# A graph network on one core: the preparation in another order, thresholds inside the norm's steps, and one visit instead of two for a gathered block's rows

## The chip, the cores and the metric

The kernel runs on one core of a Trainium2 chip. The metric is the device time of one execution in microseconds (us). TensorE is called PE (its weight loads PEld), VectorE DVE, ScalarE ACT, GpSimd POOL, SyncE SP.

## The reference

A layer norm without gain and bias, a ReLU, four rounds of "add the neighbours, then a small network", and the input added back. There are N = 6250 nodes with C = 256 channels and E = 100000 edges, sorted by their target `dst`.

```python
def agg(h):
    return jax.ops.segment_sum(h[src], dst, num_segments=N)
for l in range(NL - 1):                      # NL = 4
    h = x + agg(x)
    h = relu(h @ W1s[l] + b1s[l])
    h = relu(h @ W2s[l] + b2s[l])
    x = h @ W3s[l] + b3s[l]
h = x + agg(x)
h = relu(h @ cW1 + cb1)                      # 256 to 256
h = relu(h @ cW2 + cb2)                      # 256 to 64
return h @ cW3 + cb3                         # 64 to 256

# around it
h = relu(layernorm(x))
return x + gnn(h, ...)
```

## The kernel before

All is float32 in and out. The 6250 nodes are 49 blocks of 128 (`NT`). Since no nonlinearity stands between one layer's third product and the next layer's first, these two weights are multiplied ahead (`fused`, W3 times W1), and what a layer stores to its `table` in DRAM is already multiplied for the next aggregation. The work with sorted edges is in `sorted_edges`; a second way, for unsorted edges, is behind a condition and isn't run.

An aggregation is done in two ways. For most blocks a matrix of edge counts (source by target, uint8) is multiplied with the node table that stands in SBUF. For the blocks in `gone` the table's rows are gathered by GpSimd with an indirect DMA (L1382, one DMA for 128 rows, 17 of them a block, `T = 17`), and PE sums them with one-hot matrices `hot` (L1402) in narrow products of 32 targets (L1419). There are 82 such sums over the four layers (23, 20, 20, 19), with 391, 340, 340 and 323 gathers.

*Preparation* (0 to 126 us). Three generators are stepped by hand, so that the order of their `next` calls is the order of the instructions on each engine's queue:

- `look` works out where edges start. It loads every 128th target (L620, cast at L644), counts how many lie below each of 98 half blocks (L652 to L661), gathers for each half block the near edges (L663, 1408 of them, `NEAR`), and counts those below 17 thresholds 4 nodes apart: 11 on DVE (L695) and 6 on ACT by a sign with a sum (L698, `Sign`), ahead of the norm. From the counts it works out `first` and `starts` (L704 and on) and queues 32 gathers (`asks`), which `ask(n)` issues. Later stages build `idx` (the sources to gather) and `rel` (targets relative to the block).
- `normed` is the layer norm over 25 pairs of blocks in 30 steps: x loads in groups of 6 blocks, `moments` (L879), square roots for 6 blocks at a time (L885), `scale` (L899), transposes (L908), the product with the first weights (L920), and the table's parts `XY` (L936, L940).
- `fused` makes the products of weights, with a copy of a bias on POOL (L579).

`load_biases` issues bias loads on ACT's queue (L538, L541), and `load_w` the weights (L527). `wrong` is a small tile in which flags of unsorted edges are collected; it is cleared on DVE (L640).

*Layer 0* (from 126 us). `build` makes the count matrices: per step two one-hots, `lo` and `hi` (L1035, DVE), two products (L1076), and a cast of the counts to uint8, in turn on ACT (L1084) and DVE (L1086). The first `PRE` = 12 ticks of two steps run before the first product of the layer (to 142.7 us). Layer 0 then multiplies node block by node block (L1588), and stores the matrices, which layers 1 to 3 load again panel by panel (L1665).

*Gathered blocks* (class `Gathered`). A planner counts the time of the work issued on PE in a clock of its own (`clock`). A layer's gathers are issued evenly over it (`flow`, `send`), starting `LEAD` = 21 ahead of the first visit, into 24 buffers in layer 0 and 25 after it. A "visit" is a group of the L1419 products between two stretches of other products. `ROUNDS` gives two visits to a block: rows `c + 4 m` with c in (3, 1, -1), then with c in (0, 4, 2). `hot` has two buffers; that of the next visit is made right behind a visit. After a block's second visit, `finish` adds the sums to the block (L1448) and goes on with its small network.

The planner's price of a visit is `VISIT` = 1.7.

Of the kernel before, what the change touches and what calls it, by code (L numbers as in the profile page):

```python
# [8 lines left out]
F32 = mybir.dt.float32  # L9
# [387 lines left out]
def sorted_edges(  # L397
# [59 lines left out]
    ROUNDS = ((3, 1, -1), (0, 4, 2))  # L457
# [3 lines left out]
    NEAR = 11 * P  # L461
# [36 lines left out]
    rel = const.tile([P, left[NQ] // T, len(ROUNDS), 3, P // Q], BF16, name="rel")  # L498
# [58 lines left out]
    def fused(pool, w3_aps, w1_aps):  # L557
# [11 lines left out]
        for l in range(NLAYER):  # L569
# [8 lines left out]
            b3b = pool.tile([P, KC, P], F32, name="b3b", bufs=1)  # L578
            nc.gpsimd.tensor_copy(b3b, b3[l][:, :, None].to_broadcast([P, KC, P]))  # L579
            yield  # L580
            w = pool.tile([P, KC + 1, C], F32, name="w31", bufs=1)
            for i in range(KC + 1):
                ps = ps_m.tile([P, W], F32, name="ps")
                for k in range(KC):
                    left = w3t[:, k, i * P:(i + 1) * P] if i < KC else b3b[:, k, :]
                    nc.tensor.matmul(ps[:, :C], left, w1[:, k, :], start=(k == 0),
                                     stop=(k == KC - 1))
                nc.scalar.copy(w[:, i, :], ps[:, :C])
# [28 lines left out]
    def look(pool):  # L617
        firsts_i = pool.tile([1, EB], I32, name="near_i", bufs=1)
        with nc.allow_non_contiguous_dma(reason="each tile's first destination"):
# [6 lines left out]
        nc.sync.dma_start(out=run[:FULL, :], in_=bass.AP(tensor=dst.tensor, offset=dst.offset,  # L626
                                                         ap=[[EC, FULL], [1, EC + 1]]))
        nc.sync.dma_start(out=run[FULL:FULL + 1, :E - FULL * EC],
                          in_=dst[FULL * EC:E].rearrange("(o e) -> o e", o=1))
# [15 lines left out]


        half = pool.tile([P, 2], F32, name="half", bufs=1)
        junk = pool.tile([P, NEAR], BF16, name="junk", bufs=1)
        for h in range(2):
# [3 lines left out]
                             start=True, stop=True)  # L653
            nc.vector.tensor_scalar(junk[:NSUB, e0:e1], ps[:NSUB, :e1 - e0], low[:NSUB, 0:1], None,
# [11 lines left out]
        )  # L666
        yield
# [24 lines left out]
        DV = 11  # L692
        for q in range(GSUB + 1):
            if q < DV:
                nc.vector.tensor_scalar(junk[:NSUB], near[:NSUB], float(GD * q), None,  # L695
                                        op0=OP.is_lt, op1=OP.add, accum_out=less[:NSUB, q:q + 1])
            else:
                nc.scalar.activation(junk2[:NSUB], near[:NSUB], AF.Sign, bias=edge[:NSUB, q:q + 1],  # L698
                                     accum_out=less[:NSUB, q:q + 1])
                yield  # L700
        nc.vector.tensor_scalar(less[:NSUB, DV:], less[:NSUB, DV:], -0.5, float(NEAR // 2),
                                op0=OP.mult, op1=OP.add)
        first = pool.tile([P, GSUB + 1], F32, name="first", bufs=1)
        nc.vector.tensor_scalar(first[:NSUB], less[:NSUB], at[:NSUB, 0:1], None, op0=OP.add)  # L704
        starts = pool.tile([NSUB, GSUB], I32, name="starts", bufs=1)
        nc.vector.tensor_scalar(starts, first[:NSUB, :GSUB], float(E - P), None, op0=OP.min)
        wd = pool.tile([P, GSUB, P], I32, name="wd", bufs=1)
        ws = pool.tile([P, GSUB, P], I32, name="ws", bufs=1)
        for q in range(GSUB):
            for w, e in ((wd, dst), (ws, src)):  # L710
                asks.append((w[:NSUB, q, :], e, starts[:, q:q + 1]))
        ask(4)
# [4 lines left out]
        sel = pool.tile([P, NQ, PW], F32, name="near_i", bufs=1)  # L717
# [100 lines left out]
        for w, (q0, q1) in ((3, (0, NQ - 1)), (4, (NQ - 1, NQ))):  # L818
            rows = gone[q0][1] * T
            nc.vector.tensor_reduce(wrong[:rows, w:w + 1], off[:rows, q0:q1, :],  # L820
                                    axis=mybir.AxisListType.XY, op=OP.max)
        ask(len(asks))
# [8 lines left out]
        yield  # L831
        for t, o in ((fd, rel), (fs, idx)):
# [4 lines left out]
            if o is rel:  # L837
                v = ps[:, :left[NQ]].rearrange("p (b k) -> p b k", k=T)
                for i, rounds in enumerate(ROUNDS):
                    for c in rounds:  # L840
                        g = 1 if c < 0 else 0
                        nc.vector.tensor_scalar(o[:, :, i, (c - min(rounds)) // 2, g:],
# [16 lines left out]
    def normed(pool, ps_t, ps_z):  # L859
        G = 6  # L860
# [91 lines left out]
        settle(G)  # L952
        yield
        for s in range(len(pairs) + 5):
            if s % (G // 2) == 0 and s and s * 2 + 3 * G < NT:
                load(s * 2 + 3 * G)
            for lag, f in ((3, out), (4, high), (0, scale), (1, turn), (2, times), (-G, moments),
                           (4, low), (5, keep)):
                if 0 <= s - lag < len(pairs) and (f is not moments or s - lag >= G):
                    f(s - lag)  # L960
            settle(s + G - 1)
            yield

    with tc.manual_schedule():
        with tc.tile_pool(name="prep", bufs=2) as prep, tc.tile_pool(
# [5 lines left out]
            next(rows)  # L971
            make_identity(nc, ident)
            nc.vector.memset(eps, EPS)
            turn_biases, (b1, b2, b3) = load_biases(prep)
            ahead_w = fused(prep, [W3s[l] for l in range(NLAYER)],
                            [W1s[l + 1] for l in range(NLAYER - 1)] + [cW1])
            next(ahead_w)
            next(looked)
            for t, pattern in ((cols, [[1, NT], [STEP, GD]]), (lanes, [[1, P]]), (colf, [[1, P]])):
                nc.gpsimd.iota(t, pattern=pattern, base=0, channel_multiplier=0,  # L980
                               allow_small_or_imprecise_dtypes=True)
            next(looked)
            next(rows)
# [70 lines left out]
        def build(hots, ats, ps_b):  # L1054
# [7 lines left out]
            for k, (s, q0) in enumerate(batches):  # L1062
# [6 lines left out]
                for q in range(0, BATCH, 2):  # L1069
# [13 lines left out]
                    if step % 2:  # L1083
# [251 lines left out]
        class Gathered:  # L1335
            def __init__(self, l):
# [11 lines left out]
                self.rows, self.us = {}, []  # L1348
# [49 lines left out]
            def one_hots(self, v):  # L1398
                g, rounds = self.visits[v]
                shape = [P, len(rounds), P // Q, Q]  # L1400
                self.hot = work.tile(shape, F32, name="hot", bufs=2)
# [6 lines left out]
            def add(self):  # L1408
# [4 lines left out]
                if v == 0:  # L1413
                    self.one_hots(0)
                end = rounds == ROUNDS[-1]
                for c in rounds:
                    for m in range(P // Q):
                        if c + 4 * m >= 0:
                            nc.tensor.matmul(  # L1419
                                self.sums[m * Q:(m + 1) * Q, :C],  # L1420
                                self.hot[:, (c - min(rounds)) // 2, m, :], self.rows[g, c + 4 * m],
# [367 lines left out]
```

## Time and profile before

| | us |
|---|---|
| median of 3 runs | 2130.42 |
| lowest and highest | 2127.44, 2132.5 |
| the profiled execution | 2135.8 |
| its span in the trace | 2134.0 |
| its granted clock of TensorE, mean | 0.988 of full |

The profile is of one execution. A line of a group reads: source line, engine, operation, output and inputs with shapes, count, then busy time in us, mean ns of one, and the engine's idle time just before, with what ended it. A line of the timeline reads: start and length in us, engine, line, operation, count, and in brackets the idle time before it and what it waited for. Windows give each engine's busy time and instruction count, the granted clock, the share of time that the DMA engines were busy, and GB/s.

### The profile page before, as it was taken

To read this page: it belongs to the slowest core of one execution; us is meant where nothing else is said; L and a number is where in the kernel's file an instruction comes from. 1 tells how busy PE (TensorE), PEld (TensorE's weight loads), DVE (VectorE), ACT (ScalarE), POOL (GpSimd) and SP (SyncE) were. 2 spreads that over 40 slices of the span, in tenths; PEclk is the share of its full clock that TensorE was granted. 3 is DMA by queue.
4 is the path that set the end of the run, shared out by engine and by line. 5 is a ranking of instruction groups with operands and counts; after the bars stand their busy time and mean duration, and the time that the engine had idled before them with its cause. 6 is when DMAs were issued, how large, how long until landed. Compare 5 with 4: busy or idle time off the path is not lost.

```text
span 2134.0 us, 33393 instructions
## 1 busy us (share of the span) xinstructions
PE 2057.4 (96%) x12076; PEld 1487.8 (70%) x12076; DVE 937.7 (44%) x2192; ACT 864.3 (41%) x1775; POOL 1445.4 (68%) x1470
## 2 busy tenths in 40 slices
PE   4979999999999999999999999999999999999997
PEld 3756766667667777777776777777776777777675
DVE  7877867667673422222233322222233433333332
ACT  4856655556556522323232433222333432223231
POOL 2727777777774477777776377777776277777773
PEclk9979999999999999999999999999999999999999
DMA  5524545545455655455455554555456555556553
GB/s 157 176 98 139 162 142 153 158 140 164 150 158 152 213 163 155 153 181 164 142 186 167 173 160 148 173 165 169 146 168 195 170 172 181 184 180 194 183 160 119
DMA packets 184901, 347.61 MB, mean 163 GB/s; under 512 B 32446, under 2 KB 118496, under 8 KB 184726
## 3 DMA queue, kind: packets, MB, share of 16 engines
q0 software_dynamic: 68960, 185.41, 29.7%
q1 hardware_dynamic: 113838, 158.12, 22.3%
q8 instruction: 97, 1.59, 0.3%
q10 hardware_dynamic: 1928, 1.85, 0.3%
q14 instruction: 78, 0.64, 0.1%
HBM read 287.98 MB, written 57.26 MB: 162 GB/s over the span
## 4 chain that ended last, share of the span: by engine, by line
PE 88%; DVE 5%; DMA 4%; issue 1%; ACT 1%; POOL 1%; SPq 0%; DVEq 0%; POOLq 0%; ACTq 0%
PE agg L1665 43%; PE agg L1588 16%; PE sums L1419 11%; PE ps L1233 6%; PE ps L1290 6%; PE bp L1076 4%; DMA rows<-table,idx 3%; PE ps L1479 1%; POOL rows L1382 1%; DVE junk L695 1%; PE bp L920 1%; DVE hi L1035 1%; DVE at L1086 1%; PE ps L1245 0%; DMA table<-zs 0%
## 5 line engine op out<-in xcount | busy, mean ns | idle before, releaser
L1382 POOL DMA_INDIRECT rows<-table,idx x1394 | 1387.7, 995 | 611.4 <-issue 220.6
L1665 PE MATMUL agg<-a,XY 128*128 128x512 f32 x4116 | 982.8, 395 | 1.9 <-DVE clT L1600 1.9
L1665 PEld LDWEIGHTS agg<-a,XY 128*128 128x128 f32 x4116 | 764.6, 188 | 209.5 <-issue 45.8
L1565 ACT CAST a<-at 128x512 fp32r<-128x512 uint8 (+1 forms) x542 | 326.9, 616 | 576.9 <-PE agg L1665 543.9
L1565 DVE CAST a<-at 128x512 fp32r<-128x512 uint8 x543 | 242.7, 448 | 552.8 <-PE agg L1665 469.3
L1588 PE MATMUL agg<-XY,a 128*128 128x512 f32 x1470 | 404.9, 409 | 1.3 <-DVE un L1600 0.7
L1588 PEld LDWEIGHTS agg<-XY,a 128*128 128x128 f32 x1470 | 258.9, 189 | 53.7 <-issue 8.7
L1419 PE MATMUL sums<-rows,hot 128*32 128x256 f32 x3772 | 256.0, 385 | 16.2 <-DMA rows<-table,idx 15.0
L1419 PEld LDWEIGHTS sums<-rows,hot 128*32 128x32 f32 x3772 | 112.6, 109 | 142.6 <-issue 53.6
L1549 ACT CAST a<-at 128x512 fp32r<-128x512 uint8 (+2 forms) x362 | 196.7, 574 | 6.5 <-PE agg L1588 6.5
L1084 ACT CAST at<-bp 128x392 uint8<-128x392 f32 x240 | 116.6, 487 | 203.7 <-PE bp L1076 191.0
L1086 DVE CAST at<-bp 128x392 uint8<-128x392 f32 x240 | 135.1, 563 | 138.2 <-PE bp L1076 138.2
L1448 DVE TENSOR_TENSOR u<-u,sums 128x256 f32<-128x256 f32 x82 | 34.3, 419 | 241.8 <-PE agg L1665 226.9
L1076 PE MATMUL bp<-hi,lo 128*128 128x196 bf16 x960 | 127.5, 255 | 11.0 <-DVE hi L1035 10.7
L1290 PE MATMUL ps<-w,h 128*128 128x256 f32 x588 | 133.9, 379 | 1.4 <-ACT h L1236 0.9
L1233 PE MATMUL ps<-h,w 128*128 128x512 f32 (+3 forms) x332 | 133.9, 545 | 0.6 <-DVE zz L1298 0.6
L1035 DVE TENSOR_TENSOR hi<-cols,pairs 128x784 bf16<-128x784 bf16 x240 | 134.3, 560 | 0.0
L1076 PEld LDWEIGHTS <-lo 128*128 128x128 bf16 x960 | 70.6, 99 | 81.9 <-DVE hi L1035 27.8
L1290 PEld LDWEIGHTS ps<-w,h 128*128 128x128 f32 x588 | 111.1, 190 | 18.7 <-ACT h L1236 1.8
L1483 ACT ACTIVATE h<-ps,bias 128x256 f32<-128x256 f32 (+1 forms) x116 | 47.2, 464 | 154.9 <-PE ps L1479 154.9
L1298 DVE TENSOR_TENSOR zz<-ps,w 128x512 f32<-128x512 f32 (+1 forms) x75 | 50.1, 678 | 117.0 <-PE ps L1290 117.0
L1035 DVE TENSOR_TENSOR lo<-lanes,pairs 128x512 bf16<-128x512 bf16 x240 | 100.3, 418 | 1.3 <-ACT pairs L1030 1.3
(171 smaller groups left out, 989.7 us busy)
## 6 DMA issues: line engine op xcount, KB each, us to landing
at<-mat SPq DMA_DIRECT2D x151, 448.0 KB
mat<-at SPq DMA_DIRECT2D x30, 784.0 KB
rows<-table,idx POOLq DMA_INDIRECT x1394
table<-zz SPq DMA_DIRECT2D x72, 256.0 KB
back<-table SPq DMA_DIRECT2D x99, 128.0 KB
xs<-in_x_dram SPq DMA_DIRECT2D x8, 768.0 KB
table<-zs SPq DMA_DIRECT2D x24, 256.0 KB
out_dram<-zz SPq DMA_DIRECT2D x24, 256.0 KB
```

The costliest lines, as they stand in the source:

```text
L1035: nc.vector.tensor_tensor(o.rearrange("p q (n t) -> p q n t", t=2), values.rearrange("p (n t) -> p n t", t=2)[:, None, :, :].to_broadcast( ...
L1076: mm = nc.tensor.matmul(bp[:, m * HW:(m + 1) * HW], lo[:, q + m, :], hi[:, q + m, :], start=True, stop=True)
L1084: nc.scalar.copy(o, v)
L1086: nc.vector.tensor_copy(o, v)
L1233: mm = nc.tensor.matmul(ps[:mp, :w], weights[l][0][:, c, i * P:i * P + mp], h1[:, c, :w], start=(c == 0), stop=(c == KC - 1))
L1290: mm = nc.tensor.matmul(o, h2[0][:, c, nodes], w3[:, c, :], start=(c == 0), stop=(c == KC - 1))
L1382: got = nc.gpsimd.indirect_dma_start(out=t, out_offset=None, in_=tables[self.l][:, :], in_offset=bass.IndirectOffsetOnAxis(ap=idx[:, o:o + ...
L1419: nc.tensor.matmul(self.sums[m * Q:(m + 1) * Q, :C], self.hot[:, (c - min(rounds)) // 2, m, :], self.rows[g, c + 4 * m], start=(c == ROUND ...
L1549: nc.scalar.copy(a[:, i * m * P:(i + 1) * m * P].rearrange("p (j d) -> p j d", j=m), counts[b][:, j:j + m, :])
L1565: cast(o, at[:, :, d:d + m * P])
L1588: mm = nc.tensor.matmul(agg, a[:, d:d + P], XY[:, j, :], start=(j == 0), stop=(j == NT - 1))
L1665: mm = nc.tensor.matmul(agg[c][:, :w], XY[:, j, o:o + P], a[:, :w], start=(j == 0 and half == 0), stop=(j == NT - 1 and half == 1))
```

## The change

- `ROUNDS` has one round of all six values of c: a gathered block is summed in one visit with 46 passes. `hot` has 6 x 4 x 32 columns and one buffer, and is made four pieces of work behind the visit (`later(4, ...)`). The planner's constants are LEAD 32 and VISIT 3.0, and a layer's first `send` is of 8 tiles.
- The near edges are 1280 for each half block. 8 thresholds are counted on DVE and 9 on ACT, one pair in each of the first steps of the norm; behind every four, `settled` works out their starts and queues their gathers.
- x is loaded for two groups first, and for two more after the first moments; moments run 4 pairs ahead, not 6. The loads of the edges `run` stand behind the gather of the near edges.
- The weights' loads stand ahead of the biases' on ACT's queue. A square root into `wrong`, ahead of its clearing on DVE, loads the ACT function table early.
- The bias copies on POOL are gone (the product reads the bias by broadcast). The products of weights are spread over the first norm steps, as are the steps of `look` (`STAGES`).
- In `build`, all casts of the first 24 steps are on ACT.

```diff
-    ROUNDS = ((3, 1, -1), (0, 4, 2))
+    ROUNDS = ((3, 1, -1, 0, 4, 2),)
-    NEAR = 11 * P
+    NEAR = 10 * P
...
-            b3b = pool.tile([P, KC, P], F32, name="b3b", bufs=1)
-            nc.gpsimd.tensor_copy(b3b, b3[l][:, :, None].to_broadcast([P, KC, P]))
...
-        DV = 11
-        for q in range(GSUB + 1):
-            if q < DV:
-                nc.vector.tensor_scalar(junk[:NSUB], near[:NSUB], float(GD * q), None,
-                                        op0=OP.is_lt, op1=OP.add, accum_out=less[:NSUB, q:q + 1])
-            else:
-                nc.scalar.activation(junk2[:NSUB], near[:NSUB], AF.Sign, bias=edge[:NSUB, q:q + 1],
-                                     accum_out=less[:NSUB, q:q + 1])
-                yield
...
-        ask(4)
+        def settled(q0, q1):
+            odd = slice(q0 + 1 - q0 % 2, q1, 2) if q1 <= GSUB else slice(q0, q1)
+            nc.vector.tensor_scalar(less[:NSUB, odd], less[:NSUB, odd], -0.5, float(NEAR // 2),
+                                    op0=OP.mult, op1=OP.add)
+            nc.vector.tensor_scalar(first[:NSUB, q0:q1], less[:NSUB, q0:q1], at[:NSUB, 0:1], None,
+                                    op0=OP.add)
+            if q1 > GSUB:
+                return
+            nc.vector.tensor_scalar(starts[:, q0:q1], first[:NSUB, q0:q1], float(E - P), None,
+                                    op0=OP.min)
+            for q in range(q0, q1):
+                for w, e in ((wd, dst), (ws, src)):
+                    asks.append((w[:NSUB, q, :], e, starts[:, q:q + 1]))
+
+        for q in range(0, GSUB, 2):
+            nc.vector.tensor_scalar(junk[:NSUB], near[:NSUB], float(GD * q), None,
+                                    op0=OP.is_lt, op1=OP.add, accum_out=less[:NSUB, q:q + 1])
+            for k in (q + 1,) if q + 2 < GSUB else (q + 1, q + 2):
+                nc.scalar.activation(junk2[:NSUB], near[:NSUB], AF.Sign, bias=edge[:NSUB, k:k + 1],
+                                     accum_out=less[:NSUB, k:k + 1])
+            if q % 4 == 2:
+                settled(q - 2, q + 2)
+            if q + 2 < GSUB:
+                yield
...
     def normed(pool, ps_t, ps_z):
-        G = 6
+        G, LEAD = 6, 4
...
-        for t0 in range(0, 4 * G, G):
+        for t0 in (0, G):
             load(t0)
         yield
-        for s in range(G):
+        moments(0)
+        yield
+        for t0 in (2 * G, 3 * G):
+            load(t0)
+        for s in range(1, LEAD):
             moments(s)
...
             next(rows)
+            ahead_w = fused(prep, [W3s[l] for l in range(NLAYER)],
+                            [W1s[l + 1] for l in range(NLAYER - 1)] + [cW1])
+            next(ahead_w)
             make_identity(nc, ident)
             nc.vector.memset(eps, EPS)
             turn_biases, (b1, b2, b3) = load_biases(prep)
-            ahead_w = fused(prep, [W3s[l] for l in range(NLAYER)],
-                            [W1s[l + 1] for l in range(NLAYER - 1)] + [cW1])
-            next(ahead_w)
+            nc.scalar.activation(wrong[:, :1], eps, AF.Sqrt)
+            next(looked)
+            next(rows)
             next(looked)
...
-            turn_biases()
-            for _ in range(2 * NLAYER):
-                next(looked)
-                next(ahead_w)
-            next(looked)
-            STAGES = (*range(4, 20, 2), 20, 22, 24)
+            STAGES = (*range(10), 10, 11, 12, 13, 15, 16, 18, 19, 20, 21, 22, 23, 24, 25, 26)
             for i, _ in enumerate(rows):
-                ask(2)
+                ask(3 if i < 9 else 2)
+                if i == 1:
+                    turn_biases()
+                if i < 2 * NLAYER + 1:
+                    next(ahead_w, None)
                 if i in STAGES:
                     next(looked, None)
...
-                    if step % 2:
+                    if step % 2 or step <= 2 * PRE:
                         nc.scalar.copy(o, v)
                     else:
                         nc.vector.tensor_copy(o, v)
...
             def begin(self):
                 self.first = clock[0] + LEAD
+                self.one_hots(0)
...
-                self.hot = work.tile(shape, F32, name="hot", bufs=2)
+                self.hot = work.tile(shape, F32, name="hot")
...
                 passed(VISIT)
                 self.done += 1
                 if self.done < self.n:
-                    self.one_hots(self.done)
+                    later(4, lambda v=self.done: self.one_hots(v))
...
-        LEAD, TAIL = 21.0, 10.0
-        COLS, FULL32, TURN, VISIT, BUILD, BURST = 0.457e-3, 1.68e-3, 0.4, 1.7, 0.2, 0.3
+        LEAD, TAIL = 32.0, 10.0
+        COLS, FULL32, TURN, VISIT, BUILD, BURST = 0.457e-3, 1.68e-3, 0.4, 3.0, 0.2, 0.3
...
-            layers[0].send(layers[0].upto[1])
+            layers[0].send(8)
```

More of the change, by code (lines that the diff above doesn't have):

```diff
@@ L666, in look @@
         )
+        nc.sync.dma_start(out=run[:FULL, :], in_=bass.AP(tensor=dst.tensor, offset=dst.offset,
+                                                         ap=[[EC, FULL], [1, EC + 1]]))
+        nc.sync.dma_start(out=run[FULL:FULL + 1, :E - FULL * EC],
+                          in_=dst[FULL * EC:E].rearrange("(o e) -> o e", o=1))
         yield
@@ L715, in look @@
+        settled(GSUB, GSUB + 1)
+        yield
         NV = 2 + len(CUTS)
         both = pool.tile([P, NV], F32, name="both", bufs=1)
-        sel = pool.tile([P, NQ, PW], F32, name="near_i", bufs=1)
+        sel = pool.tile([P, NQ, PW], F32, name="f", bufs=1)
         some = pool.tile([P, NQ, PW], F32, name="rel", bufs=1)
@@ L956, in normed @@
                 load(s * 2 + 3 * G)
-            for lag, f in ((3, out), (4, high), (0, scale), (1, turn), (2, times), (-G, moments),
+            for lag, f in ((3, out), (4, high), (0, scale), (1, turn), (2, times), (-LEAD, moments),
                            (4, low), (5, keep)):
-                if 0 <= s - lag < len(pairs) and (f is not moments or s - lag >= G):
+                if 0 <= s - lag < len(pairs) and (f is not moments or s - lag >= LEAD):
                     f(s - lag)
-            settle(s + G - 1)
+            settle(s + LEAD - 1)
             yield
```

41 lines of the change are left out of this document (20 added, 21 removed).

## The prediction

> **What bounds the kernel now.** I read the page first (busy times, chain), then the gathers by layer, the timeline of PE and POOL inside a layer, the groups of instructions, and at last the preparation in windows. On the page:
>
> ```profile
> PE 2057.4 (96%) x12076; PEld 1487.8 (70%) x12076; DVE 937.7 (44%) x2192; ACT 864.3 (41%) x1775; POOL 1445.4 (68%) x1470
> PE 88%; DVE 5%; DMA 4%; issue 1%; ACT 1%; POOL 1%; SPq 0%; DVEq 0%; POOLq 0%; ACTq 0%
> ```
>
> TensorE fills the span and the chain, so a saving on PE looks like time. But POOL issues one gather per 128 rows, and its busy share is an average over stages. The windows over the gathers alone (one per layer, from first gather to last; columns: window, length, POOL busy, count, clock, DMA share) and two neighbours in the timeline of POOL in layer 2 say more:
>
> ```profile
> 126.60:675.20 548.60, 394.65 (x391) 0.98 0.50 152
> 719.20:1164.30 445.10, 337.66 (x340) 1.00 0.56 173
> 1205.70:1648.50 442.80, 334.22 (x340) 1.00 0.56 172
> 1686.80:2106.00 419.20, 321.04 (x323) 1.00 0.58 184
> ...
> 1301.43 0.95 POOL L1382 DMA_INDIRECT rows<-table,idx  x1 [0.31 <-issue]
> 1302.68 0.95 POOL L1382 DMA_INDIRECT rows<-table,idx  x1 [0.30 <-issue]
> ```
>
> A gather is followed by 0.30 us in which POOL waits for nothing that shows. With that gap, layers 1 to 3 hold 337.66 + 340 x 0.30 = 439.7 of 445.1, 436.2 of 442.8 and 417.9 of 419.2 us: POOL has 5.4, 6.6 and 1.3 us to spare. Layer 0 has 36.7 (394.65 + 117.3 of 548.6). So in layers 1 to 3 the number of gathers sets the length, and the change leaves it as it is: 391, 340, 340 and 323. That PE is full as well there means that the two are matched, not that PE alone decides.
>
> **The merged visit, on PE.** The timeline of PE in layer 3 and layer 1 (start, length, passes):
>
> ```profile
> 715.24 22.15 PE L1665 MATMUL agg<-a,XY 128*128 128x512 f32 x96
> 737.33 2.05 PE L1419 MATMUL sums<-rows,hot 128*32 128x256 f32 x22
> ...
> 1705.85 9.38 PE L1665 MATMUL agg<-a,XY 128*128 128x512 f32 x40
> 1715.15 1.50 PE L1419 MATMUL sums<-rows,hot 128*32 128x256 f32 x24
> 1716.59 9.38 PE L1665 MATMUL agg<-a,XY 128*128 128x512 f32 x40
> 1725.89 1.50 PE L1419 MATMUL sums<-rows,hot 128*32 128x256 f32 x22
> 1727.33 3.03 PE L1665 MATMUL agg<-a,XY 128*128 128x512 f32 x12
> ```
>
> From start to start a visit takes 1.44 us with 24 passes and 1.44 with 22 recorded, and the passes stay as many (46 a block) in one visit. What goes is the change from wide to narrow products and back. From 40 products in 9.30 us and 96 in 22.09, one takes 0.228 and 0.17 is fixed per stretch; with the like on the visit's side I take 0.2 us a block (0.17 to 0.35). There are 23 blocks in layer 0 (391 / 17) and 59 behind it: 4.6 and 11.8 us.
>
> In layer 0, where POOL has room, the 4.6 us count. In layers 1 to 3 PE would come 4, 4 and 3.8 us earlier to rows that POOL still issues at 1.26 us each: the saving turns into waits. **0**, bounded by what POOL has to spare: -4, -4 and -1 = -9. On the other side, a visit that takes 17 tiles at once out of 24 or 25 buffers can hold POOL for a moment; were that a third of a gather's 1.26 us in every second visit, 59 / 2 x 0.4 = +12. I take the 0 because the spare 1 to 7 us say that POOL is hardly ever stopped.
>
> **The merged visit, on DVE.** The groups (busy, mean ns, idle before and its releasers):
>
> ```profile
> L1419 PE MATMUL sums<-rows,hot 128*32 128x256 f32 x3772 | 256.0, 385 | 16.2 <-DMA rows<-table,idx 15.0 <-DVE hot L1402 1.1
> L1402 DVE TENSOR_TENSOR hot<-colf,rel 128x384 f32<-128x384 f32 x164 | 90.0, 551 | 0.0
> L1035 DVE TENSOR_TENSOR hi<-cols,pairs 128x784 bf16<-128x784 bf16 x240 | 134.3, 560 | 0.0
> L1035 DVE TENSOR_TENSOR lo<-lanes,pairs 128x512 bf16<-128x512 bf16 x240 | 100.3, 418 | 1.3 <-ACT pairs L1030 1.3
> L1076 PE MATMUL bp<-hi,lo 128*128 128x196 bf16 x960 | 127.5, 255 | 11.0 <-DVE hi L1035 10.7 <-ACT at L1084 0.3
> L1084 ACT CAST at<-bp 128x392 uint8<-128x392 f32 x240 | 116.6, 487 | 203.7 <-PE bp L1076 191.0 <-issue 9.9 <-ACT pairs L1030 2.4
> L1086 DVE CAST at<-bp 128x392 uint8<-128x392 f32 x240 | 135.1, 563 | 138.2 <-PE bp L1076 138.2
> ```
>
> The two sizes of L1035 give 0.52 ns an element and some 150 ns fixed; with that fixed part, `hot` of 768 elements takes 0.15 + 2 x 0.40 = 0.95 us in one piece where it took 2 x 0.55. That is less in all, but one piece of 0.95 stands in front of the next `lo` and `hi`, for which PE's counting products already wait 10.7 us in layer 0: at most 10.7 / 46 = 0.23 per `hot` of today. The new piece is 0.4 longer than the old one: 23 x 0.4 = **+9** in layer 0, between nothing (it falls where DVE idles) and 23 x 0.95 = +22. I take the middle one since the waits on `hi` show that the builds have no slack there. There is one `hot` buffer now, so its operation waits for the passes of the visit before, and behind it on DVE are queued the next `lo`, `hi` and casts; it is issued four pieces of work after the visit, when those passes are over, so this wait costs nothing. In layers 1 to 3 nothing is counted and `hot` is hidden (idle of PE on it: 1.1 us in all).
>
> **The ends of the layers.** The end of layer 1 on PE's timeline:
>
> ```profile
> 1163.55 0.64 PE L1419 MATMUL sums<-rows,hot 128*32 128x256 f32 x8 [1.58 <-DMA rows<-table,idx]
> 1167.38 1.92 PE L1419 MATMUL sums<-rows,hot 128*32 128x256 f32 x10 [3.19 <-DMA rows<-table,idx]
> 1169.22 3.78 PE L1665 MATMUL agg<-a,XY 128*128 128x512 f32 x8
> ```
>
> PE waits for the last tiles, and behind the very last come 10 passes. After the change the first tiles used are 3, 7, 11 and 15, so the whole last visit waits for the last but one. From there to tile 16 stand 15 products or 30 passes, 30 x 1.44 / 24 = 1.8 us, where its row is 1.26 behind: +0.6, and the four layers together +2.4, rounded **+3** for what stands later in the order. After the 3.19 us wait 8 products took 3.78 us and not 8 x 0.228 = 1.8: a lump of waiting costs about 2 us more if it slows PE. Four ends: 0 to +11. The Trainium skill, "TensorE: Matmul & The Clock Gate", section "HAM oscillation — how this bites in real kernels", says that gaps of PE above about 3.4 us set the clock to half, and that it takes about as long to come back; here 3.19 us in one piece, with 1.58 shortly before, did so. By that rule every merged last visit pays for it, and the sum would be 8 us above mine; that is rival (4).
>
> **The start of the counting** (126.0 to 142.7 us, before the first products by node). All 24 casts go to ACT. DVE was full there (16.52 us of 16.7, below) and loses 12 x 0.563 = 6.8 us; ACT takes 24 x 0.487 + 3 copies of 0.26 = 12.5 us and becomes the bound, with 0.8 to start: 13.3 us for 16.7, **-3.4**.
>
> **The preparation.** Windows (window, length, PE, PEld, DVE, ACT, POOL busy), then groups, then single rows:
>
> ```profile
> 0.00:126.00 126.00, 91.12 (x418) 69.44 (x418) 97.42 (x275) 74.92 (x162) 57.75 (x76) 0.93 0.49 150
> 0.00:15.50 15.50, 2.92 (x4) 0.96 (x4) 2.94 (x16) 0.00 (x0) 6.12 (x26) 1.00 0.75 225
> 15.50:43.50 28.00, 15.31 (x50) 10.82 (x50) 26.91 (x63) 15.65 (x32) 1.79 (x4) 0.94 0.36 116
> 43.50:126.00 82.50, 72.89 (x364) 57.66 (x364) 67.56 (x199) 59.27 (x132) 49.83 (x47) 0.92 0.49 148
> 126.00:142.70 16.70, 9.47 (x50) 5.14 (x50) 16.52 (x39) 6.88 (x18) 7.93 (x8) 0.58 0.45 152
> ...
> L695 DVE TENSOR_SCALAR_CACHE_REDUCE junk<-near 98x1408 bf16<-98x1408 f32 x11 | 17.8, 1620 | 0.4
> L698 ACT ACTIVATE near_i<-near,edge 98x1408 bf16<-98x1408 f32 x6 | 8.8, 1474 | 2.1 <-POOL b3b L579 1.4 <-ACT w L588 0.6
> ...
> 0.99 0.06 DVE L640 MEMSET wrong<- 128x5 f32 x1
> 6.70 0.56 DVE L644 CAST near<-near_i 1x782 f32<-1x782 int32 x1 [5.64 <-DMA near_i<-in_dst_dram]
> 12.01 1.19 POOL L663 DMA_INDIRECT near_i<-in_dst_dram,at_i  x1 [8.55 <-DMA brows<-in_L_gnn_b3s_dram]
> 15.65 0.48 ACTq L527 DMA_DIRECT2D w1n<-in_L_gnn_W1s_dram  x1
> 22.80 0.94 DVE L689 TENSOR_SCALAR near<-near_i,low 98x1408 f32<-98x1408 int32 x1
> 43.48 2.08 ACT L899 ACTIVATE h<-xs,shift,rstd 128x256 f32<-128x256 f32 x4
> ```
>
> DVE sets it: 97.4 of 126 us, full from 15.5 to 43.5 with the thresholds, while the norm's first pair waits until 43.48. *Work:* 11 thresholds of 1.62 us become 8 of 1280 columns, 1.47: -6.0; near over fewer columns -0.1; four times the small steps behind the thresholds, some 10 more of 0.2: +2. DVE has about 93.3 us. ACT has 9 thresholds of 1.34 for 6 of 1.47: +3.2.
>
> *Start:* the memset of `wrong` now waits for the square root on ACT, and that for all DMA issues ahead of it, the weights' and the biases'; the last of these went out at 15.65. Behind the memset on DVE stands the cast of the first edges (L644), so it moves from 6.70 to about 16, and the gather of the near edges behind it from 12.0 to about 21; its POOL gather, the run's loads behind it on SP, and the near conversion (22.80) follow. The moments of the first pairs stand ahead of that, so the norm's first pair comes at about 25, not 43.5.
>
> *The eight steps with thresholds:* ACT has 59.27 / 25 = 2.4 us a pair from the last window, 1.5 for a threshold and some 0.7 of the weights' products: 4.6 a step, 37 us, to 62. DVE has in them 8 x 1.5 + 2 + 8 x 67.56 / 25 = 35.6 us of work, as much as ACT. *The rest* is 93.3 - 2.9 - 7 (15.5 to 25) - 35.6 = 47.8 us of DVE work, at the 82% of the third window 58 us: end at 120, were the two engines never to wait for each other in the eight steps. They do: each step's threshold pair, moments and turns go back and forth in a fixed order, and the copy that one waits for stands behind the other's 1.5 us threshold. (The x loads and the run's loads trade places on SP, and the three `b3b` copies leave POOL: nothing waits there that is not waiting for DVE already.) At 75% for DVE the eight steps take 47 us instead of 37: end at 130, or **+4**, with +1 for the chain from the last thresholds to the edges' lists, whose steps stand later in the norm than now: **+5**. Ends: -12 (no waits in the eight steps, and 90% of DVE after them: 62 + 53 = 115, 114 rounded), +12 (70% and 75%).
>
> **Sum** against the profiled execution of 2135.8 us: preparation +5, start of counting -3.4, visits in layer 0 -4.6, `hot` +9, layers 1 to 3 0, ends +3 = +9, so 2144.8. The profile stands 5.4 us above the median of the runs, 2130.4; there it is **2139**.
>
> **Rivals.** *(1) Faster, the overlap pays:* DVE has 28.6 idle us in the preparation, 12.6 of them ahead of 15.5, and the norm may fill those that the thresholds' serial stretch made. Then -12 there, `hot` hidden but for +3, -3.4 and -4.6, ends +1: -16, **2114**. It decides where DVE is above 90% busy from 25 us on. For it: PE and ACT idle half of 15.5 to 43.5. Against it: DVE doesn't.
> *(2) No change:* the waits of POOL were PE's, and go: -9 in layers 1 to 3, sum 0, **2130**. For it: PE is full in these layers too. Against it: the gathers follow each other at 1.26.
> *(3) Much slower:* a visit takes 17 of 24 or 25 buffers at once, and POOL stops at each. At 0.4 us for 59 visits this is +24 on the +9: **2163**. For it: the buffers hardly hold more than one block. Against it: the first tile is asked for 32 us ahead, not 21, and the last of a visit 32 - 16 x 1.3 = 11 us, before 21 - 7 x 1.3 = 12.
> *(4) Slower by the clock:* at each layer's end the two waits become one, and PE runs at half speed behind it: 4 x 2 = 8 us on the +9, **2147**. For it: the row of 3.78 us. Against it: that end has the loss already, so not all four can be new.
>
> **Chances.** Forecast 0.43, (1) 0.25, (2) 0.16, (3) 0.07, (4) 0.09. A measurement tells this kernel from no change at about 0.2%, 4.3 us. Slower: the forecast, (3) and (4), 0.59, of which 0.03 fall into "same" at the forecast's lower end; (2) gives 0.13 to "same" and 0.03 to faster. So faster 0.28, same 0.16, slower 0.56. Range: from (1), 2114, to 2154, which is the forecast with `hot` at its 22 (2152) and a little of (4); it leaves out (3). Both signs hold much of it, and the forecast's own range is 2130 (`hot` at nothing) to 2152.
>
> **What would show it.** The first norm row (L899's) near 25 us and DVE's cast of the first edges behind 15 us; the first adjacency cast at 131, not 126; a `hot` of 0.95 us and a longer wait of L1076 on `hi`; first to last gather 445, 443 and 419 us as before, with more PE idle on rows. Gather windows shorter by 4 us or more make me wrong towards (2); an end of the preparation before 120 towards (1); POOL idle beyond 10 us in a layer towards (3).

## The result: 2139.95 us, 0.4% slower

The changed kernel takes 2139.95 us (median of 5 runs, 2139.82 to 2142.23), before 2130.42 (5 runs, 2127.44 to 2135.63). The ratio is 1.0039 with a 95% interval of 1.0025 to 1.0054. The forecast was 2139, slower.

The page of the changed kernel, busy times and chain:

```profile
PE 2038.6 (95%) x12076; PEld 1499.0 (70%) x12076; DVE 920.6 (43%) x2103; ACT 867.3 (41%) x1794; POOL 1449.6 (68%) x1467
PE 84%; DVE 5%; DMA 3%; issue 1%; ACT 1%; POOL 1%; DVEq 0%; SPq 0%; POOLq 0%; ACTq 0%
```

TensorE works 18.8 us less than before (2057.4; 2055.9 in the kernel with the new preparation alone, further down), about what the merged visits were to save, and the kernel is longer all the same. What it waits for, before and after (waited for, us in total, times, longest), first in the profile before:

```profile
PE sums L1419 <- DMA rows<-table,idx: 15.0, 12, 3.3
PE bp L1076 <- DVE hi L1035: 10.7, 22, 1.8
```

and in the profile after:

```profile
PE sums L1442 <- DMA rows<-table,idx: 30.3, 15, 4.3
PE bp L1096 <- DVE hi L1055: 13.4, 25, 3.0
```

The waits on gathered rows grew by 15.3 us: most of the saving of TensorE stands there. GpSimd, which issues the gathers, has no time left. Its waits for TensorE in layer 1 (720 to 1165 us), first in the profile before, then after:

```profile
POOL rows L1382 <- PE agg L1665: 39.9, 120, 1.9
POOL rows L1403 <- PE agg L1688: 35.6, 117, 0.3
```

A pause of 0.3 us follows every gather, whatever it is put down to. Before, 5 pauses in layer 1 and 13 in layer 2 are longer, 5.6 and 9.2 us in all; after, none inside layers 1 to 3 is longer. The windows over the gathers of each layer, after:

```profile
130.50:681.50 551.00, 393.41 (x391) 0.98 0.50 151
723.60:1167.70 444.10, 340.81 (x340) 0.99 0.56 174
1208.30:1647.70 439.40, 336.10 (x340) 1.00 0.56 174
1686.60:2107.50 420.90, 322.78 (x323) 0.99 0.58 180
```

Against 548.6, 445.1, 442.8 and 419.2 before: layer 0 is longer, layers 1 to 3 together only 2.7 us shorter. The preparation now ends at about 131.4 us, not 126. Its windows after (window, length, then PE, PEld, DVE, ACT, POOL busy):

```profile
0.00:15.50 15.50, 0.00 (x0) 0.00 (x0) 0.22 (x2) 0.00 (x0) 2.76 (x12) 1.00 0.75 217
15.50:29.80 14.30, 6.51 (x16) 3.08 (x17) 8.97 (x38) 3.40 (x7) 3.36 (x14) 1.00 0.44 141
29.80:70.00 40.20, 29.64 (x128) 22.22 (x126) 29.16 (x84) 33.95 (x69) 20.88 (x21) 0.98 0.47 134
70.00:131.40 61.40, 53.52 (x276) 42.48 (x277) 55.24 (x160) 41.01 (x93) 30.31 (x27) 0.93 0.42 134
131.40:144.30 12.90, 9.44 (x51) 5.10 (x50) 11.56 (x28) 11.10 (x28) 8.48 (x8) 0.56 0.57 189
```

VectorE has 93.59 us of work up to 131.4 (97.42 before) and does almost none of it ahead of 15.5. In the stretch of the thresholds (29.8 to 70) it is 73% busy and ScalarE 84%. Behind it VectorE is 90% busy. How the late start comes about is in the timeline:

```profile
16.84 1.28 ACT L996 ACT_TABLE_LOAD   x1 [16.84 <-DMA brows<-in_L_gnn_cb_dram]
18.14 0.20 ACT L996 ACTIVATE wrong<-eps 128x1 f32<-128x1 f32 x1
18.39 0.55 DVE L639 CAST near<-near_i 1x782 f32<-1x782 int32 x1 [17.35 <-issue]
23.69 1.19 POOL L660 DMA_INDIRECT near_i<-in_dst_dram,at_i  x1 [20.23 <-DVE stats L893]
26.85 1.09 ACT L913 ACTIVATE h<-xs,shift,rstd 128x256 f32<-128x256 f32 x2 [1.03 <-DVE shift L906]
28.89 0.89 DVE L690 TENSOR_SCALAR near<-near_i,low 98x1280 f32<-98x1280 int32 x1 [0.49 <-DMA near_i<-in_dst_dram,at_i]
```

The square root stands behind the bias loads on ScalarE's queue, the clearing of `wrong` behind the square root, and the first edges' cast behind that on VectorE's queue: 18.39 instead of 6.70 us.

### The profile page after: what moved, and what is told of

It is laid out like the page before. It is cut to its first block, busy times and chain, and to the rows that moved or that the text cites. A ratio compares the mean times of both kernels' runs of the same rounds, so it can differ in the third digit from the quotient of the medians.

```text
span 2138.1 us, 33269 instructions
## 1 busy us (share of the span) xinstructions
PE 2038.6 (95%) x12076; PEld 1499.0 (70%) x12076; DVE 920.6 (43%) x2103; ACT 867.3 (41%) x1794; POOL 1449.6 (68%) x1467
## 3 DMA queue, kind: packets, MB, share of 16 engines
q0 software_dynamic: 68960, 185.36, 29.8%
## 4 chain that ended last, share of the span: by engine, by line
PE 84%; DVE 5%; DMA 3%; issue 1%; ACT 1%; POOL 1%; DVEq 0%; SPq 0%; POOLq 0%; ACTq 0%
PE agg L1688 42%; PE agg L1611 13%; PE sums L1442 11%; PE ps L1253 6%; PE ps L1310 6%; PE bp L1096 3%; DMA rows<-table,idx 3%; PE ps L1502 1%; DVE hi L1055 1%; POOL rows L1403 1%; DVE at L1106 1%; DVE lo L1055 1%; DVE hot L1426 1%; PE ps L1245 0%; ACT at L1104 0%
## 5 line engine op out<-in xcount | busy, mean ns | idle before, releaser
L1442 PE MATMUL sums<-rows,hot 128*32 128x256 f32 x3772 | 248.5, 390 | 30.4 <-DMA rows<-table,idx 30.3
L1442 PEld LDWEIGHTS sums<-rows,hot 128*32 128x32 f32 x3772 | 123.7, 111 | 146.8 <-DMA rows<-table,idx 41.8
L1104 ACT CAST at<-bp 128x392 uint8<-128x392 f32 x252 | 121.5, 490 | 192.4 <-PE bp L1096 184.2
L1106 DVE CAST at<-bp 128x392 uint8<-128x392 f32 x228 | 128.3, 563 | 141.7 <-PE bp L1096 141.7
L1096 PE MATMUL bp<-hi,lo 128*128 128x196 bf16 x960 | 127.6, 256 | 14.6 <-DVE hi L1055 13.4
```

What stands on the lines that cost most here:

```text
L1096: mm = nc.tensor.matmul(bp[:, m * HW:(m + 1) * HW], lo[:, q + m, :], hi[:, q + m, :], start=True, stop=True)
L1104: nc.scalar.copy(o, v)
L1106: nc.vector.tensor_copy(o, v)
L1442: nc.tensor.matmul(self.sums[m * Q:(m + 1) * Q, :C], self.hot[:, c - min(rounds), m, :], self.rows[g, c + 4 * m], start=(c == ROUNDS[0][0] ...
```

## The experiments

The kernel before ran beside each set on the same chip. It takes 2130.5 and 2130.9 us on the two chips on which most of the runs below were made (either is called the usual chip), and 2365 and 2362 us on two others (the slower chips); there only the ratio to the kernel before on the same chip is used, and comparisons within traces. Medians from start to start and of visits are worked out from the start times in the traces.

**The merged visit alone.** The kernel before with these edits and what goes with them (`rel`, `hot`, first `send`):

```diff
-    ROUNDS = ((3, 1, -1), (0, 4, 2))
+    ROUNDS = ((3, 1, -1, 0, 4, 2),)
-                self.hot = work.tile(shape, F32, name="hot", bufs=2)
+                self.hot = work.tile(shape, F32, name="hot")
-        LEAD, TAIL = 21.0, 10.0      # and VISIT 1.7
+        LEAD, TAIL = 32.0, 10.0      # and VISIT 3.0
```

> The kernel before with only the merged visit and the planner's constants that go with it (LEAD, VISIT, first send); the preparation and the casts are those of before. Theory (the gathers hold layers 1 to 3, the one-piece hot delays the counting in layer 0): visits -4.6, hot +9, ends of layers 0 to +3, so +4.4 to +7.4 on before, 2135 to 2138. Rival A (TensorE is the bound in all layers): -16 of visits, so 2123 or less even with the hot. Rival B (the whole loss is in the preparation): 0, 2130.

Measured: 2135.75 us, ratio 1.0026 (1.0016 to 1.0036), +5.2. The theory's range holds it, both rivals are out. Its gather windows:

```profile
126.10:680.30 554.20, 392.23 (x391) 0.98 0.49 150
722.40:1166.50 444.10, 340.75 (x340) 0.99 0.55 174
1207.10:1645.70 438.60, 335.28 (x340) 1.00 0.55 174
1685.00:2104.50 419.50, 321.36 (x323) 1.00 0.57 181
```

Layer 0 is 5.6 us longer than in the profile before; layers 1 and 2 are 1.0 and 4.2 shorter, layer 3 is 0.3 longer. The saving and the waits are the merged visit's alone (its page and its list of waits):

```profile
PE 2039.6 (96%) x12076; PEld 1500.1 (70%) x12076; DVE 929.6 (44%) x2110; ACT 858.9 (40%) x1775; POOL 1446.7 (68%) x1470
...
PE sums L1422 <- DMA rows<-table,idx: 29.0, 17, 4.3
```

**The preparation alone.** The kernel after with the two visits, buffers and constants of before (the edits above, reversed).

> The kernel after with the two visits per block of before, their two hot buffers and the planner's constants of before; preparation and casts are those of after. Theory: preparation +5, casts -3.4: +1.6, 2132. Rival A: the merged visit saved 16 us and the preparation cost some 25: 2155. Rival B (the whole loss is in the preparation): +9.5, 2140.

Measured: 2136.11 us, ratio 1.0022 (1.0012 to 1.0032), +5.6. The theory said +1.6, so the preparation costs more than forecast; rival B is out too, for with +5.2 of the visits it makes 2141.4, close to the 2139.95 of both together.

**The casts alone.** In the kernel before:

```diff
-                    if step % 2:
+                    if step % 2 or step <= 2 * PRE:
```

> The kernel before with one edit: all casts of the first 24 counting steps on ScalarE. Theory: the stretch before the first product by node loses 3.4 us, nothing behind it changes: 2127. Rival: ScalarE and VectorE were not the bound of it, 0: 2130.

Measured: 2127.94 us, -2.6, ratio 0.9990 (0.9980 to 1.0001). From the first to the 24th cast it is 11.2 us, before 14.9: the 3.7 of the trace are there, as forecast, while the ratio alone doesn't exclude no change. Without the casts, then, the preparation costs 2136.1 - 2127.9 = 8.2 us by the medians and 6.8 by the two ratios, with some 3 us either way from their intervals.

**Before, once more.**

> The kernel before once more, for a second profile: the first one stands 5.4 us above the median of its runs, and the two profiles differ by 4.2 us where the medians differ by 9.5. If the first profile was a long execution, this one is near 2130 and shows which stretch was long; if the profiler adds it always, it is near 2136.

Measured: 2125.64 us, span 2123.8. The first cast of counts marks the end of the preparation. The one line's view (count, shortest, median and longest ns, first and last start) in the profile of before, and in this one:

```profile
L1084 ACT CAST at<-bp x240: 485/485/523, 127.4 to 650.1; 128x392 uint8<-128x392 f32 x120
```

```profile
L1084 ACT CAST at<-bp x240: 485/485/523, 122.5 to 645.4; 128x392 uint8<-128x392 f32 x120
...
0.00:122.50 122.50, 85.53 (x422) 65.45 (x423) 98.45 (x279) 75.04 (x163) 58.24 (x77) 0.99 0.51 156
```

The same program prepares in 122.5 or 127.4 us; the two other runs with this preparation (the merged visit alone, the casts alone) have the first cast at 127.6 and 127.3. The granted clock of the preparation was 0.99 in the short one (second line, a window) and 0.93 in the long one, and TensorE was busy 5.6 us less in the short one; that goes with it, and no run here shows what causes it. Behind the preparation the two differ by 5 us more: from the first product by node to the end it is 1986.1 and 1991.3 us. The two spans differ by 10.2 us, and their mean, 2128.9, is 9.2 below that of the changed kernel: one profile of a kernel is not its median.

**The square root into a tile of its own.** In the kernel after, so that VectorE's start waits for nothing on ScalarE:

```diff
-            nc.scalar.activation(wrong[:, :1], eps, AF.Sqrt)
+            nc.scalar.activation(const.tile([P, 1], F32, name="warm"), eps, AF.Sqrt)
```

> The kernel after, with the early square root on ScalarE written to a tile of its own instead of the flags' tile, so that VectorE's clearing of the flags, and the first edges' cast behind it, wait for nothing on ScalarE. Theory (the late start of VectorE is most of what the preparation costs): the cast of the first edges moves from 18.4 to about 7 us, the near edges come some 8 us earlier, the norm's first pair still waits for the first moments and the table load at 18 us: 4 to 7 us less, 2133 to 2136. Rival (ScalarE's and VectorE's steps with thresholds set the time from the first pair on, the start does not matter): 0, 2140.

This set ran on a slower chip, where before takes 2365.05. Measured: 2396.19, ratio 1.0136 (1.0112 to 1.0159). The time can't be set beside 2139.95. In the trace the first cast of counts came at 124.8 us, against 132.0 after, and 132.2 in a later run of the same preparation on the usual chip: the 7 us come in the preparation, as the theory says, and the norm's first pair at 19.1 and not 26.8.

**`hot` in two halves**, in the kernel after (the second two pieces of work behind the first):

```diff
+                part(0)
+                self.rest_hot = [lambda: part(3)]
+                later(2, self.rest_of_hot)
```

> The kernel after, with hot made in two operations of 384 columns, the second two pieces of work behind the first. Theory (one piece of 0.95 us in front of lo and hi delays the counting): the longer piece's cost goes, -4 to -8 in layer 0, 2132 to 2136. Rival (the total of VectorE's work counts, not the piece): two operations take 2 x 0.55 for 0.95, 23 x 0.15 = +3.5, 2143.

In the same set: 2407.3, ratio 1.0186 (1.0163 to 1.0208). The kernel after itself was not run on that chip, so the effect of the halves stays open.

**No `hot` in layer 0**, in that set and, since it told nothing there, in another:

```diff
-                if self.hots >= v:
+                if self.hots >= v or self.l == 0 and v:
```

> The kernel after, which leaves out the making of hot in layer 0 after the first visit (the old one is used again, so the sums of layer 0 are not the reference's). Theory (hot costs 9 us in layer 0): 2131. Rival (hot is hidden there; layer 0 is longer because of waits on rows): 2139 to 2140.

2405.32, ratio 1.0179 (1.0161 to 1.0197): inconclusive on that chip. The second run:

> The kernel after, which leaves out the making of hot in layer 0 after the first visit (the sums of layer 0 are not the reference's); once more, beside a before of about 2130. Theory (hot costs 9 us in layer 0): 2131, and the stretch from the 24th cast to the last gather of layer 0 shorter by 9 of its 538 us. Rival (hot is hidden; layer 0 is longer because of waits on rows): 2139 to 2140, 538 us.

Measured: 2131.6 us, ratio 0.9998 (0.9987 to 1.0009), 8.3 below the kernel after; from the 24th cast to the last gather of layer 0 530.5 us for 538.3. Its window over layer 0, and TensorE's waits:

```profile
130.70:673.90 543.20, 389.98 (x391) 0.99 0.51 153
...
PE sums L1442 <- DMA rows<-table,idx: 27.3, 15, 4.3
PE bp L1096 <- DVE hi L1055: 9.2, 18, 3.1
```

So all of `hot` in layer 0 behind the first visit costs 8 us. The forecast's 9 was for something else, for what one piece costs more than two halves; that is taken up below. TensorE's windows behind the first stretch of counting, after and in this run (length, then busy time):

```profile
144.30:681.50 537.20, 526.02 (x3518) 372.40 (x3518) 366.05 (x828) 320.82 (x739) 384.03 (x383) 0.99 0.50 151
144.40:673.90 529.50, 523.62 (x3518) 371.71 (x3518) 347.58 (x806) 320.06 (x737) 381.09 (x383) 1.00 0.51 153
```

Of the 7.7 us, 5.3 are idle time of TensorE (11.2 and 5.9), nearly all of it waits on `hi` (8.6 and 3.9 us between 144 and 675), and 2.4 are busy time of the same products, at a granted clock of 0.99 and 1.00. The waits on rows hardly change: they are in the other layers.

**Less work of TensorE in layers 1 to 3.** In the kernel after, tried twice:

```diff
-                        if c + 4 * m >= 0:
+                        if c + 4 * m >= 0 and (self.l == 0 or c != 0):
```

> The kernel after, which leaves out 8 of the 46 passes of each visit in layers 1 to 3 (the four products of c = 0), with all gathers kept: 59 x 8 x 0.06 = 28 us less work of TensorE. Theory (the gathers hold these layers): 0 to -5, so 2135 to 2140, and the gathers of layers 1 to 3 as long as before. Rival (TensorE is the bound there): 2112.

> The kernel after, which leaves out 8 of the 46 passes of each visit in layers 1 to 3 (the products of c = 0; their sums are not the reference's), with all gathers kept: 59 x 8 x 0.06 = 28 us less work of TensorE; once more, beside a before of about 2130. Theory (the gathers hold these layers): 0 to -5, so 2135 to 2140, first to last gather of layers 1 to 3 at 444, 439 and 421 us, less at most 2 each. Rival (TensorE is the bound there): 2112, 435, 430 and 412.

Both fell on slower chips: 2394.13 (ratio 1.0131, 1.0112 to 1.0151) and 2400.95 (1.0155, 1.0126 to 1.0183). There a visit is slowed in another way (last section), so that this test stays open. The next two runs hold a part of the answer in another form.

**The preparation with an early start**, with the visits of before:

```diff
-            nc.scalar.activation(wrong[:, :1], eps, AF.Sqrt)
+            nc.scalar.activation(const.tile([P, 1], F32, name="warm"), eps, AF.Sqrt)
...
-            nc.scalar.dma_start(out=rows[r:r + n, :c], ...)
+            nc.gpsimd.dma_start(out=rows[r:r + n, :c], ...)
```

> A kernel with the visits of before and the preparation and casts of after, and two more edits: the early square root goes to a tile of its own, and the bias loads are issued by GpSimd instead of ScalarE, so that ScalarE is free at about 5 us and not at 17. Theory (the preparation of after loses by its late start): the alone-standing preparation measured +5.6 over before with its casts; the start of VectorE gives back 7, ScalarE's start another 0 to 5: 2124 to 2129, at or below before. Rival (the steps with thresholds set the time, however early they start; the casts alone gain): 2133 to 2136.

Measured: 2136.92 us, ratio 1.0027 (1.0017 to 1.0037). The preparation ends at 124.0 by its first cast, 7.2 earlier than in the preparation alone (131.2), but the time is no better. Its gather windows and its group of panel products:

```profile
123.30:670.30 547.00, 395.04 (x391) 0.98 0.50 152
716.60:1166.60 450.00, 332.23 (x340) 1.00 0.56 171
1207.20:1655.00 447.80, 329.63 (x340) 1.00 0.55 170
1691.20:2103.60 412.40, 313.71 (x323) 1.00 0.59 184
...
L1685 PE MATMUL agg<-a,XY 128*128 128x512 f32 x4116 | 1001.9, 399 | 1.9 <-DVE clT L1620 1.9
```

In the preparation alone this group is:

```profile
L1685 PE MATMUL agg<-a,XY 128*128 128x512 f32 x4116 | 981.8, 395 | 1.8 <-DVE clT L1620 1.8
```

The gather windows of layers 1 to 3 there:

```profile
720.10:1164.90 444.80, 337.14 (x340) 1.00 0.55 173
1204.40:1647.40 443.00, 334.30 (x340) 1.00 0.55 172
1683.80:2103.50 419.70, 321.46 (x323) 1.00 0.58 184
```

Layers 1 and 2 are 5 us longer, layer 3 is 7 shorter, and the products themselves are slower: from start to start 0.234 us each (median) and not 0.227. The new tile of 4 bytes a partition had moved the tiles allocated behind it, `a`, `u` and the rows of layer 0 among them, from a multiple of 128 bytes to 32 behind one.

**The same without the tile.**

```diff
-            nc.scalar.activation(const.tile([P, 1], F32, name="warm"), eps, AF.Sqrt)
+            nc.scalar.activation(colf[:, :1], eps, AF.Sqrt)
```

> The kernel of the run before (visits of before, preparation and casts of after, early start of VectorE and ScalarE), but the early square root goes into the first column of colf, which GpSimd fills later, so that no tile is added. In the run before, the added tile moved every tile that is allocated behind it (a, u, lo, rows of layer 0) by 32 bytes, and layers 1 and 2 took 5 us more each, with TensorE's products 398 ns instead of 394 and no new waits on its side. Theory (the shift of the addresses made TensorE slower): layers 1 and 2 as in before (445 and 443 us), 2124 to 2129. Rival (the biases on GpSimd's queue, or the preparation's new order in some other way, lengthen the layers): 2134 to 2138 again.

On a slower chip: 2354.24, before there 2361.6, ratio 0.9969 (0.9957 to 0.9982). So it beats the kernel before, casts included, on the chip where it was run; on the usual one it was not run. The products take 0.227 us from start to start again. On the other slower chip the kernel with the tile (square root in a tile of its own) had 0.234 and the three others of its set, without it, 0.227. So the added tile was the cause of the slower products; that it is by the moved addresses is the reading left, since nothing else about them is known to have changed.

The run with the tile, beside the preparation alone, answers from the other side what less work of TensorE was to answer. It has 20.1 us more of panel products by the groups above, some 7 in each of layers 1 to 3, but from the first product by node to the end it took 1999.2 us instead of 1990.9, only 8 us more. The layers differ. In layers 1 and 2 the 7 us of work lengthen the gather windows by 5 each: there TensorE was the bound, and GpSimd's longer pauses grew from 6.0 and 9.5 us to 20.1 and 23.7. Layer 3 has as much more work and is 7.3 us shorter. A gather took 0.971 us in it (313.71 / 323) and not 0.995; with the 0.3 of the pause 323 of them make 411 and 418 us, near the 412.4 and 419.7 of the windows, and TensorE's waits on rows there went from 6.9 us to none. So layer 3 goes by the gathers. Why a gather was faster in this kernel no run here shows.

## Right or wrong, point by point

- **What bounds.** Right for the changed kernel: it has 18.8 us less work of TensorE and 15.3 more of waits on rows, and inside layers 1 to 3 GpSimd has no pause above 0.3 us. The term was 0; the merged visit alone shows -1.0, -4.2 and +0.3 in the gather windows, inside the -9 that the spare time of POOL allowed, and a part that the sum left out. With two visits the engines were only matched: in layers 1 and 2 more work of TensorE did cost time (the shifted tiles), in layer 3 the gathers set it.
- **The visit.** A merged one takes 2.73 us in the median, two halves 2 x 1.43, so 0.13 a block by the visits alone. TensorE's busy time fell by 17.3 us beside the kernel with the same preparation, 0.21 for each of 82 blocks (forecast 0.2).
- **`hot`.** 951 ns in one piece (forecast 0.95). All of it costs 8 us in layer 0; the forecast of 9 was for one piece against two halves, which no run shows by itself. An estimate: from the 24th cast to the last gather layer 0 takes 537.9 and 538.3 us with merged visits, 532.9 to 534.9 with two, and the visits of its 23 blocks save at least 3.0, so the piece costs at least 6 us more, and no more than the 8. The waits on `hi` grew as forecast, but the 10.7 us on which the forecast leaned were mostly ahead of the first product by node: behind it (144 to 675 us) they were 3.4 before and are 8.6 after.
- **Start of the counting.** -3.7 by the trace (forecast -3.4).
- **Preparation.** The mechanism is right: the cast of the first edges behind 15 us (18.39), the first pair near 25 (26.85), VectorE's work 93.6 (93.3), 73% busy among the thresholds (75%). On the profile on which the sum was made the size is right too: +5 forecast, the first cast 4.6 later (127.4 and 132.0). By the medians it is +8.2, with some 3 us either way. A short preparation, as the 122.5 in one of the four profiles, would pull the median of before down and was not in the sum; how often it comes no run here shows. The upper end of the range, at 70% and 75%, is +14 by the prediction's own figures and not +12.
- **Ends of the layers.** The last visit waits for the last but one tile, as forecast. The end of layer 1, after:

```profile
1163.20 1.06 PE L1442 MATMUL sums<-rows,hot 128*32 128x256 f32 x2 [4.32 <-DMA rows<-table,idx]
1168.22 5.33 PE L1442 MATMUL sums<-rows,hot 128*32 128x256 f32 x40 [3.96 <-DMA rows<-table,idx]
1173.48 2.35 PE L1688 MATMUL agg<-a,XY 128*128 128x512 f32 x8
```

  The 40 passes after the 3.96 us wait take 5.33 us, at a granted clock of 0.50, where 46 take 2.73 inside a layer. The Trainium skill, "TensorE: Matmul & The Clock Gate", section "HAM oscillation — how this bites in real kernels", says that idle gaps above about 3.4 us drop the clock; the trace agrees here. It shows no sharp border, though: in the last layer 3.15 us were enough (40 passes in 4.28 at a clock of 0.63), while before, at the end of layer 2, a wait of 3.28 us left the clock at 1.00. Rival (4) is thus right in its mechanism, but the products behind take 2.35 us now and 3.78 before: the loss moved more than it grew. From the last gather of layer 1 to the first of layer 2 it is 40.6 us, before 41.4. Behind the last gather the kernel needs 2.6 us more (30.6 and 28.0), near the +3; with the changes from layer to layer (-1.9, -0.8 and +0.6) it is +0.5 in all.
- **Rival (1)** decides at 90% of VectorE. It reached that, but only behind 70 us; the 15.3 us without work ahead of 15.5 and the 11.0 among the thresholds were not in it. With the start mended, the preparation comes 7 us earlier, and with the casts it then beats before on a slower chip, the one on which it was run.
- **Sum.** +9 forecast, +9.5 by the medians, but only +4.1 between the two profiles on which its terms can be measured:

| term | forecast | between the profiles |
|---|---|---|
| preparation (first cast) | +5 | +4.6 |
| start of the counting | -3.4 | -3.7 |
| layer 0, to its last gather | -4.6 + 9 | +5.4 |
| gathers of layers 1 to 3 | 0 | -2.7 |
| from layer to layer, and the end | +3 | +0.5 |

  The forecast for the profile was 2144.8 and it was 2139.95. The first profile of before stood 5.4 us above its median, that of after at its median; the forecast took the 5.4 off for both. So that the median came within 1 us is partly luck: layers 1 to 3 and the ends were 5 us too high, and the profile before 5 us too long. Two profiles of the same kernel differ by 5 us behind the preparation, so no term of the table is good to better than a few us.

## What to carry to other kernels

When two engines are matched, work saved on one turns into its waits on the other, while work added on either can cost time: count the waits on the rows before counting the saving. A cheap early instruction (here a square root to load a table) takes with it whatever writes the same tile, so look at what stands ahead of it on its queue. Take a second profile before pricing a few us by one, and check that an added tile does not move the others.

## What the runs showed of the hardware

- **An address off by 32 bytes.** Tiles that TensorE streams (fp32r, 512 columns), moved from a multiple of 128 bytes to 32 behind one, took 0.234 us a product instead of 0.227, 3%, on the usual chip and on a slower one. In layer 0, where TensorE streams `XY`, which did not move, it is 0.235 beside 0.233. Other distances were not tried.
- **Long rows of short narrow passes that slow down on some chips.** On the slower chips before takes 11% more. Two visits in `hot` in halves there:

```profile
1138.00 4.03 PE L1454 MATMUL sums<-rows,hot 128*32 128x256 f32 x46
1158.40 1.89 PE L1454 MATMUL sums<-rows,hot 128*32 128x256 f32 x24
1161.09 0.38 PE L1454 MATMUL sums<-rows,hot 128*32 128x256 f32 x1 [0.79 <-issue]
1161.82 0.40 PE L1454 MATMUL sums<-rows,hot 128*32 128x256 f32 x1 [0.36 <-issue]
```

  In the second visit, past its first 24 passes, single passes follow each other every 0.7 us, waiting for nothing that the profile shows; the median of a merged visit there is 4.2 to 5.2 us (2.73 on the usual chip), that of a half visit 1.43 on both kinds. So 24 passes in a row get through and 46 often don't: there the merged visit costs more, and the runs with it have ratios of 1.013 to 1.019. What causes it is open. A late supply of instructions would fit "issue", but no packet of the queues of kind "instruction" moves during this stall (the nearest end at 1153.50 and start at 1174.65 us).
